# Eleven distances in the order in which two graphs' pieces are given out, and layer 3's projections as one block

## The chip, the cores and the metric

The kernel runs on one core of a Trainium2 chip. The metric is the time of one execution on the device, in microseconds (us); the median of several runs is given. A core has five engines that run side by side, each through its own queue of instructions: TensorE (PE, matrix products), VectorE (DVE), ScalarE (ACT), GpSimd (POOL) and SyncE (SP, which here issues transfers). Transfers are also issued by POOL.

## The reference

Sixteen graphs, each with 1024 nodes of 256 numbers (x) and a 1024 by 1024 adjacency, go through four graph layers. Every layer takes a normalized copy of x, cut at zero, and adds its result to x:

```python
h = jnp.maximum(_layernorm(x, axis=-1), 0.0)
x = x + layer(h, adj, ...)
```

- Layers 0 and 1 are attention with one head. h is multiplied by a weight matrix W; a logit for each edge is leaky_relu(f1[i] + f2[j]) with f1 and f2 linear in h; a softmax runs over the edges (along the first axis in layer 0, along the second in layer 1); the result is elu(attention @ (h W)).
- Layer 2 is a mean over the neighbours of h W_msg, plus h W_upd and a bias, cut at zero.
- Layer 3 is attention with four heads of 64 columns, with a bias, a cut at zero, the head's own projection added, and a normalization over each head's 64 columns.

## The kernel before, in words

**One graph.** Its nodes lie in eight tiles of 128 (NT = 8). `graph(b)` runs through the graph's stages. First come the statistics and the normalized rows of x (`Norm.pair`, four pairs of tiles): ACT writes `hn` (L667), PE transposes it (`pt_h`, L680), ACT copies it into `ht` (L681). Along with these go the mask steps: `Mask.step` turns a piece of the transposed adjacency (`raw`, loaded by SP in 256 KB pieces, L566) into bytes on ACT (L575); three pieces are loaded ahead, and each step loads another. Then, for each of the layers:

- *Layer 0* (`layer0`): eight projections (PE L686, ACT L746), each with a mask step; then a row of exponentials is spread over all partitions: a transpose `ps_col` (L699), `e_row` on ACT (L703), a transfer to DRAM (`d_row`, L705) and one back to all partitions (`row`, L711), both issued by SP. Eight tiles of attention weights `p` follow (DVE L769 and L771), and eight outputs (PE L759), each of which ACT reads twice (exponential L791, copy L793) and DVE adds to x (L736, L737, in `residual`). `residual` also gathers the sums for the next layer's norm: after every second output DVE makes `shift` (L635), ACT the squares `unread` (L640), and after every fourth POOL the inverse deviations `rs` (L592, L593).
- *Layer 1* (`layer1`): the same with projections read by ACT L802, a scaling of `hs` by ACT (L820), one DVE operation for each `p` (L822) and outputs L815, read by ACT L838 and L840.
- *Layer 2* (`layer2`): its norm needs a scale for each row; so `Norm.settle` makes `scales` on DVE (L657, L658) once `rs` is there, and only then ACT makes `hn`. This is done once before the seventh output of layer 1 (in `residual`) and once before layer 2. Eight projections are split into `hi` and `lo` (L869 to L872), and eight outputs multiply them by the adjacency (L877, L883), whose pieces POOL loads (L585).
- *Layer 3* (`layer3`): eight projections (ACT L906, and for each pair DVE L913 and L914), a wait, then four heads. A head takes one row (`row3`, of which two are held) and eight `p` (DVE L929); of each pair of `p` PE makes 32 products of 64 columns (L942). ACT reads the result (L950).
- *The tail* (`tail`): eighteen pieces, mostly DVE operations on half of the graph, two squares on ACT (L976), `rs` on POOL, and the stores.

**Two or three graphs at a time.** Every stage is a Python generator. Each `yield` gives a distance in planned units, that is, how much later the generator's next piece is given out. A queue merges the generators by these times; graph b starts at b * 120, so the heads and the tail of one graph lie among layers 0 and 1 of the next:

```python
APART = 120.0
...
while queue:
    queue.sort(key=lambda g: g[:2])
    at, b, g = queue.pop(0)
    try:
        queue.append((at + next(g), b, g))
```

`loads(b)` is a generator of its own: it issues the loads of x on POOL (`load_x`, L545, 512 KB each), and 30 units later the first three mask loads on SP. `more()` loads the weights of layers 1, 2 and 3 in the same way; those transfers are held back by `behind` (L484), a small DVE copy out of the newest layer-0 `p` of the first graph.

The order in which pieces are given out is the program's order. The framework that builds the kernel sorts the instructions of each engine's queue, with program order as the priority. Instructions marked `later` keep the program's order among themselves: all of SP's transfers, the first matmuls of layer 0's first two outputs, and some of the tail.

Of the kernel before, what the change touches and what calls it, by code (L numbers as in the profile page):

```python
# [421 lines left out]
def tile_simple_stack(  # L422
# [12 lines left out]
    B, N, D = x.shape  # L435
# [9 lines left out]
    S, S3 = 0.2, 0.01  # L445
    W3 = D + 2 * H
    HW = HO + 1
    STEP = 1.54
    EARLY = 2

    const = ctx.enter_context(tc.tile_pool(name="const", bufs=1))
# [290 lines left out]
    def layer0(b, xs, m, norm, after):  # L742
        hs = new_hs()
        for n in range(NT):
            ps = project(norm, wx[0], n, D + 2)
            nc.scalar.activation(hs[:, n, : D + 2], ps[:, : D + 2], AF.Copy, scale=norm.rs[n])  # L746
            m.step()
            yield 0.9
        mask = m.bytes
        row_a, row_b = [everywhere(d, "row") for d in spread(column(hs[:, :, D : D + 1], 1), 1, (1.0, S), "l0")]  # L750
        q = small.tile([P, NT], F32, tag="q", name="q")
        nc.scalar.activation(q, hs[:, :, D + 1], AF.Exp, scale=1.0 - S)
        watch(b, 0, hs[:, :, D : D + 2])
        yield 6.38
        ps_ = []
        early = [at_ps.tile([P, HALF], F32, tag="at", name="ps_o0") for _ in range(EARLY)]

        def product(ps, i, j):
            m = nc.tensor.matmul(  # L759
                ps[:, :D], ps_[j][:, i * P : (i + 1) * P], hs[:, j, :D], start=(j == 0), stop=(j == NT - 1)  # L760
            )
            if i < EARLY and j < 7:
                later(m)

        for j in range(NT):
            if m.raws:
                m.step(2)
            p = weights("p0")
            nc.vector.scalar_tensor_tensor(p, row_a, q[:, j : j + 1], row_b, op0=OP.mult, op1=OP.max)  # L769
            z = small.tile([P, 2], F32, tag="z", name="z", bufs=8)  # L770
            nc.vector.scalar_tensor_tensor(p, p, 1.0, mask[:, j, :], op0=OP.mult, op1=OP.mult, accum_out=z[:, 0:1])  # L771
            nc.vector.reciprocal(z[:, 1:2], z[:, 0:1])
            nc.scalar.activation(hs[:, j, :D], hs[:, j, :D], AF.Copy, scale=z[:, 1:2])  # L773
            ps_.append(p)
            if b == 0:
                gates.append(p)
            for i, ps in enumerate(early):
                if j:
                    product(ps, i, j - 1)
            yield 2.6  # L780
        for i, ps in enumerate(early):
            product(ps, i, NT - 1)
        for i in range(NT):
            if i < EARLY:
                ps = early[i]
            else:
                ps = at_ps.tile([P, HALF], F32, tag="at", name="ps_o0")
                for j in range(NT):
                    product(ps, i, j)
            e = work.tile([P, D], F32, tag="e", name="e")  # L790
            nc.scalar.activation(e, ps[:, :D], AF.Exp)  # L791
            v = work.tile([P, D], F32, tag="v", name="v")
            nc.scalar.copy(v, ps[:, :D])  # L793
            residual(xs, i, v, after, e)
            yield 3.9


    def layer1(b, xs, mask, norm, after):
        hs = new_hs()
        for n in range(NT):  # L800
            ps = project(norm, wx[1], n, D + 2)
            nc.scalar.activation(hs[:, n, : D + 2], ps[:, : D + 2], AF.Copy, scale=norm.rs[n])  # L802
            yield 1.05
        (d_row,) = spread(column(hs[:, :, D + 1 : D + 2], 1), 1, (S - 1.0,), "l1")
        row = everywhere(d_row, "row")
        watch(b, 1, hs[:, :, D : D + 2])
        q = small.tile([P, NT], F32, tag="q", name="q")
        nc.scalar.activation(q, hs[:, :, D], AF.Exp, scale=1.0 - S)
        nc.scalar.activation(hs[:, :, D], hs[:, :, D], AF.Exp, scale=S)
        yield 5.0  # L810
        ps_ = []
        early = [at_ps.tile([P, HALF], F32, tag="at", name="ps_o1") for _ in range(EARLY)]

        def product(ps, i, j):
            nc.tensor.matmul(  # L815
                ps[:, : D + 1], ps_[j][:, i * P : (i + 1) * P], hs[:, j, : D + 1], start=(j == 0), stop=(j == NT - 1)
            )

        for j in range(NT):
            nc.scalar.activation(hs[:, j, :D], hs[:, j, :D], AF.Copy, scale=hs[:, j, D : D + 1])  # L820
            p = weights("p1")
            nc.vector.scalar_tensor_tensor(p, row, q[:, j : j + 1], mask[:, j, :], op0=OP.max, op1=OP.mult)  # L822
            ps_.append(p)
            for i, ps in enumerate(early):
                product(ps, i, j)
            yield 1.3
        for i in range(NT):
            if i < EARLY:
                ps = early[i]
            else:  # L830
                ps = at_ps.tile([P, HALF], F32, tag="at", name="ps_o1")
                for j in range(NT):
                    product(ps, i, j)
            k = b * NT + i
            z = shares[:, k : k + 1]
            nc.vector.reciprocal(z, ps[:, D : D + 1])
            e = work.tile([P, D], F32, tag="e", name="e")
            nc.scalar.activation(e, ps[:, :D], AF.Exp, scale=z)  # L838
            v = work.tile([P, D], F32, tag="v", name="v")
            nc.scalar.activation(v, ps[:, :D], AF.Copy, scale=z)  # L840
            residual(xs, i, v, after, e)
            yield 3.74
# [55 lines left out]
    def layer3(b, xs, mask, norm, res):  # L898
# [5 lines left out]
        for n in range(NT):  # L904
            ps = project(norm, wx[3], n, W3)
            nc.scalar.activation(hs[:, n, :], ps[:, :W3], AF.Copy, scale=norm.rs[n])  # L906
            if n % 2:
                pair = slice(n - 1, n + 1)
                nc.scalar.activation(hbv[:, pair, :, HO], terms[:, pair, H:], AF.Exp, scale=S3)
                t = hbv[:, pair, :, :HO]  # L910
                hv = hs[:, pair, :D].rearrange("p t (h e) -> p t h e", e=HO)
                bias = rows["bias3"].rearrange("p (h e) -> p h e", e=HO).unsqueeze(1).to_broadcast([P, 2, H, HO])
                nc.vector.tensor_tensor(t, hv, bias, op=OP.add)  # L913
                nc.vector.tensor_tensor(t, t, hbv[:, pair, :, HO:].to_broadcast([P, 2, H, HO]), op=OP.mult)  # L914
            yield 1.15
        d_row = spread(column(terms[:, :, :H], H), H, (S3 - 1.0,), "l3")
        row = everywhere(d_row[0], "row3")
        watch(b, 2, terms)
# [35 lines left out]
    def tail(b, xs, hs, res):  # L954
# [4 lines left out]
        for g in range(NHALF):  # L959
# [6 lines left out]
            nc.vector.tensor_tensor(o, o, rz.unsqueeze(2).to_broadcast([P, PER * H, HO]), op=OP.mult)  # L966
            yield STEP
            nc.vector.tensor_tensor(of, of, hs[:, t, :D].rearrange("p t (h e) -> p t h e", e=HO), op=OP.add)
            yield STEP
            nc.vector.tensor_reduce(m[:, 0, :], o, axis=AX.X, op=OP.add)  # L970
            yield STEP
            total = m[:, 0, :].unsqueeze(2).to_broadcast([P, PER * H, HO])
# [10 lines left out]
        for t, o, of, m, sq in halves:  # L983
            nc.vector.tensor_reduce(m[:, 1, :], sq, axis=AX.X, op=OP.add)
            rs.append(inv_std(m[:, 1, :], PER * H, 1.0 / HO, 1e-6))
            yield STEP
        for g, (t, o, of, m, sq) in enumerate(halves):
# [18 lines left out]
    def graph(b):  # L1006
        xs = loaded.pop(b)
        m = masks.pop(b)
        norm = Norm()
        for g in range(NT // 2):  # L1010
            norm.pair(xs, g)
            m.step()
            yield 2.66
        for layer, inputs in ((layer0, (m,)), (layer1, (m.bytes,)), (layer2, ())):
            yield 2.36
            norm.settle()
            norm.flip()
            after = Norm(degrees(b) if layer is layer1 else None)
            yield from layer(b, xs, *inputs, norm, after)
            norm = after  # L1020
        yield 1.44
        norm.flip()
        res = state.tile([P, NT, H, HW], F32, tag="res", name="res", bufs=1)
        hs = yield from layer3(b, xs, m.bytes, norm, res)
        return tail(b, xs, hs, res)
# [3 lines left out]
    def loads(b):  # L1029
        loaded[b] = load_x(b)  # L1030
        yield 30.0
        masks[b] = Mask(b)
        yield 0


    APART = 120.0
    def more():

        weights01(1, w1, w1_t, a1, (1, 0))
        yield 21.6  # L1040
        weights2()
        yield 10.0
        weights3()
        yield 0

# [1 line left out]
    next(loads_0)  # L1047
    weights01(0, w0, w0_t, a0, (0, 1), wait=False)
    next(loads_0)
    queue = [(32, 0, more())] + [(b * APART, b, graph(b)) for b in range(B)] + [(b * APART - 80, b, loads(b)) for b in range(1, B)]  # L1050
    while queue:
        queue.sort(key=lambda g: g[:2])
        at, b, g = queue.pop(0)
# [86 lines left out]
```

## Time and profile before

| what | value |
|---|---|
| median of 3 runs | 2629.38 us (2628.99 to 2631.85) |
| the profiled execution | 2620.4 us, its span 2618.6 us |
| PE busy | 2473.6 us, 94% |
| DVE busy | 1965.5 us, 75% |
| ACT busy | 1448.0 us, 55% |
| POOL busy | 438.4 us, 17% |
| layer 3's `p` (L929, DVE) | 512 instructions, 1278 ns each |
| the tail's squares (L976, ACT) | 32 instructions, 1053 ns each (median) |

The profile is of one execution. Its durations add up to its own 2620.4 us, which is 9.0 us below the median of the runs. "L929" is line 929 of the kernel. "PE" is the matrix product and "PEld" the loading of its weights, which runs beside it. A wait is told as "who <- whom", with the time in total, how often, and the longest.

### The profile page before, as it was taken

The numbers are of one execution on the slowest core, as the hardware profiler recorded it, in microseconds if no ns is written. First come the engines' busy times: TensorE is split into PE (matmuls) and PEld (weight loads), VectorE is DVE, ScalarE is ACT, GpSimd is POOL, SyncE is SP. The second block draws the span as 40 slices with busy tenths as digits, with TensorE's granted clock in tenths as the row PEclk, the third lists the DMA queues.
The fourth block names the chain that finished last, engine by engine and source line by source line (L and its number), as shares of the span: only waits on it lengthen the run. The fifth ranks groups of instructions, "written<-read, shape, count | busy, mean of one in ns | idle before, by whom it ended". The sixth has DMA issues, their size and how long they took to land.

```text
span 2618.6 us, 62976 instructions
## 1 busy us (share of the span) xinstructions
PE 2473.6 (94%) x26194; PEld 2100.8 (80%) x26194; DVE 1965.5 (75%) x3815; ACT 1448.0 (55%) x4065; POOL 438.4 (17%) x454
## 2 busy tenths in 40 slices
PE   5899999999999999999999999999999999999985
PEld 4688788888878888788888878888888888878864
DVE  4357778787777877778787777977778787777858
ACT  4564755637565474755637565473755637555350
POOL 1020211203112030211202112030211203111021
PEclk7899999999999999999999999999999999999997
DMA  4531351616217161251616217161351616216021
GB/s 153 117 85 55 93 110 58 125 59 142 66 51 152 65 127 55 91 113 58 125 55 141 70 54 149 66 125 54 99 105 58 125 57 140 70 49 126 26 65 36
DMA packets 212633, 233.76 MB, mean 89 GB/s; under 512 B 10416, under 2 KB 161072, under 8 KB 212336
## 3 DMA queue, kind: packets, MB, share of 16 engines
q0 software_dynamic: 137728, 83.90, 19.4%
q1 hardware_dynamic: 74608, 145.73, 17.1%
q8 instruction: 208, 3.41, 0.5%
q14 instruction: 89, 0.73, 0.1%
HBM read 212.35 MB, written 17.24 MB: 88 GB/s over the span
## 4 chain that ended last, share of the span: by engine, by line
PE 51%; DVE 16%; ACT 15%; DMA 9%; issue 7%; POOL 2%; SPq 0%; DVEq 0%; POOLq 0%; ACTq 0%
PE ps_o L759 16%; PE ps_proj L686 11%; PE ps_o L942 11%; PE ps_o L883 6%; DVE p L929 5%; DVE p L822 4%; ACT hn L667 4%; DMA row<-d_row 3%; DMA raw<-in_adj_t 3%; ACT mask L575 2%; PE pt_h L680 2%; ACT unread L640 2%; PE ps_o L877 2%; PE ps_o L815 2%; POOL rs L593 2%
## 5 line engine op out<-in xcount | busy, mean ns | idle before, releaser
L929 DVE SCALAR_TENSOR_TENSOR p<-row,q,mask 128x1024 f32<-128x1024 f32 x512 | 632.9, 1278 | 60.8 <-PE ps_o L942 51.0
L942 PEld LDWEIGHTS ps_o<-hb,p 128*64 128x64 f32 x16384 | 506.9, 139 | 96.0 <-issue 44.7
L942 PE MATMUL ps_o<-hb,p 128*64 128x65 f32 x16384 | 544.7, 224 | 19.2 <-DVE p L929 6.1
L686 PE MATMUL ps_proj<-wx,ht 128*128 128x258 f32 (+2 forms) x2048 | 517.3, 392 | 6.5 <-ACT hs L746 5.0
L759 PE MATMUL ps_o<-hs,p 128*128 128x256 f32 x2048 | 495.6, 387 | 16.5 <-ACT hs L773 15.9
L815 PE MATMUL ps_o<-hs,p 128*128 128x257 f32 x2048 | 498.1, 390 | 13.0 <-ACT mask L575 7.4
L759 PEld LDWEIGHTS ps_o<-hs,p 128*128 128x128 f32 x2048 | 381.1, 193 | 70.2 <-ACT hs L773 21.5
L815 PEld LDWEIGHTS ps_o<-hs,p 128*128 128x128 f32 x2048 | 374.0, 191 | 69.3 <-ACT mask L575 7.6
L686 PEld LDWEIGHTS ps_proj<-wx,ht 128*128 128x128 f32 x2048 | 360.0, 190 | 85.7 <-ACT hs L746 16.0
L592 POOL TENSOR_SCALAR rs<-mv 128x4 f32<-128x4 f32 (+1 forms) x112 | 33.7, 301 | 1561.4 <-ACT unread L640 1546.8
L736 DVE SCALAR_TENSOR_TENSOR xs<-e,xs 128x256 f32<-128x256 f32 x256 | 108.0, 422 | 237.3 <-ACT e L791 164.0
L593 POOL TENSOR_TENSOR rs<-rs,neg_half 128x4 f32<-128x4 f32 (+2 forms) x144 | 257.3, 1790 | 10.7
L667 ACT ACTIVATE hn<-xs,shift 128x256 f32<-128x256 f32 x384 | 176.8, 500 | 128.3 <-DVE shift L635 126.7
L680 PE MATMUL pt_h<-ident,hn 128*128 128x128 f32 x1024 | 183.6, 285 | 37.9 <-ACT hn L667 36.5
L950 ACT ACTIVATE res<-ps_o 128x260 f32<-128x260 f32 x128 | 48.7, 381 | 298.6 <-PE ps_o L942 298.2
L883 PE MATMUL ps_o<-hi,adj 128*128 128x258 f32 x1024 | 201.2, 320 | 2.4 <-DMA adj<-in_adj 2.3
L680 PEld LDWEIGHTS pt_h<-ident,hn 128*128 128x128 f32 x1024 | 118.3, 141 | 105.6 <-ACT hn L667 85.8
L575 ACT ACTIVATE mask<-raw 128x512 uint8<-128x512 int32 x256 | 160.5, 627 | 71.8 <-DMA raw<-in_adj_t 70.6
L585 POOL DMA_DIRECT2D adj<-in_adj x128 | 114.5, 895 | 486.2 <-PE ps_o L883 452.8
L737 DVE SCALAR_TENSOR_TENSOR xs<-v,xs 128x256 f32<-128x256 f32 x384 | 160.5, 421 | 19.6 <-DVE xs L736 0.5
L769 DVE SCALAR_TENSOR_TENSOR p<-row,q 128x1024 f32<-128x1024 f32 x128 | 159.8, 1269 | 19.7 <-DMA row<-d_row 19.7
L883 PEld LDWEIGHTS ps_o<-hi,adj 128*128 128x128 f32 x1024 | 150.8, 190 | 18.3 <-DMA adj<-in_adj 4.8
(108 smaller groups left out, 3005.4 us busy)
## 6 DMA issues: line engine op xcount, KB each, us to landing
raw<-in_adj_t SPq DMA_DIRECT2D x256, 256.0 KB
adj<-in_adj POOLq DMA_DIRECT2D x128, 512.0 KB, 5.6
row<-d_row SPq DMA_DIRECT2D x112, 512.0 KB
xs<-in_x POOLq DMA_DIRECT2D x32, 512.0 KB, 7.8
out<-xs SPq DMA_DIRECT2D x32, 512.0 KB
wx<-in_w SPq DMA_DIRECT2D x3, 256.0 KB
d_row<-e_row SPq DMA_DIRECT2D x48, 4.0 KB
wts<-in_w_t SPq DMA_DIRECT2D x2, 256.0 KB
```

Source lines behind the costliest of these rows:

```text
L575: nc.scalar.activation(self.bytes[:, n, g * HALF : (g + 1) * HALF], raw, AF.Square, accum_out=squares[:, k : k + 1])
L593: nc.gpsimd.tensor_tensor(rs[:, :n], rs[:, :n], neg_half[:, :n], op=OP.pow)
L667: nc.scalar.activation(hn, xs[:, 2 * g + k, :], AF.Relu, scale=scale, bias=bias)
L680: nc.tensor.transpose(pt[:, c, k * P : (k + 1) * P], hn[:, c * P : (c + 1) * P], ident)
L686: nc.tensor.matmul(ps[:, :width], norm.ht[:, c, n * P : (n + 1) * P], w[:, c, :width], start=(c == 0), stop=(c == DC - 1))
L737: nc.vector.scalar_tensor_tensor(x, v, 0.0, x, op0=OP.max, op1=OP.add, accum_out=after.sums[:, i % 2 : i % 2 + 1])
L759: m = nc.tensor.matmul(ps[:, :D], ps_[j][:, i * P : (i + 1) * P], hs[:, j, :D], start=(j == 0), stop=(j == NT - 1))
L769: nc.vector.scalar_tensor_tensor(p, row_a, q[:, j : j + 1], row_b, op0=OP.mult, op1=OP.max)
L815: nc.tensor.matmul(ps[:, : D + 1], ps_[j][:, i * P : (i + 1) * P], hs[:, j, : D + 1], start=(j == 0), stop=(j == NT - 1))
L883: nc.tensor.matmul(ps[:, : D + 2], adj_n[j][:, i, :], h[:, i, : D + 2], start=False, stop=(h is lo and i == NT - 1), skip_group_check=True,)
L929: nc.vector.scalar_tensor_tensor(p, row, q[:, jj, h : h + 1], mask[:, jj, :], op0=OP.max, op1=OP.mult)
L942: nc.tensor.matmul(pss[g][part, k * HW : (k + 1) * HW], ps_[t][:, i * P : (i + 1) * P][:, part], hbv[:, j + t, h, :], start=(j == 0 and t ...
```

## The change

Twelve numbers are changed, eleven distances between pieces and one lead (of the loads before their graph); no operation is added or taken away. The eight projections of layer 3 are given out 0.69 apart instead of 1.15. Layer 1 waits 8.0 instead of 5.0 between its projections and its first `p`, layer 0 5.42 instead of 6.38. The other distances within the layers move by 4 to 9%. The loads of a graph are given out 60 units ahead of it instead of 80, so its first mask loads come 30 units ahead instead of 50. The weights of layers 1 to 3 start at 36 instead of 32.

```diff
@@
-    STEP = 1.54
+    STEP = 1.48
@@
-            yield 0.9
+            yield 0.98
-        yield 6.38
+        yield 5.42
@@
-            yield 2.6
+            yield 2.7
@@
-            yield 3.9
+            yield 3.74
@@
-        yield 5.0
+        yield 8.0
@@
-            yield 1.3
+            yield 1.35
@@
-            yield 1.15
+            yield 0.69
@@
-            yield 2.66
+            yield 2.55
@@
-        yield 10.0
+        yield 9.2
@@
-    queue = [(32, 0, more())] + [(b * APART, b, graph(b)) for b in range(B)] + [(b * APART - 80, b, loads(b)) for b in range(1, B)]
+    queue = [(36, 0, more())] + [(b * APART, b, graph(b)) for b in range(B)] + [(b * APART - 60, b, loads(b)) for b in range(1, B)]
```

Ahead of each pair of lines in this order: STEP (the tail), layer 0's projections, layer 0's wait for its row, layer 0's `p`, layer 0's outputs, layer 1's wait for its row, layer 1's `p`, layer 3's projections, the statistics of the first norm, the distance from layer 2's weights to layer 3's, and the queue's start (`more` and `loads`).

## The prediction

> **What bounds the kernel now.** The page comes first. TensorE (PE) is busy in 94% of the span, no other engine above 75%.
> ```profile
> PE 2473.6 (94%) x26194; PEld 2100.8 (80%) x26194; DVE 1965.5 (75%) x3815; ACT 1448.0 (55%) x4065; POOL 438.4 (17%) x454
> PE   5899999999999999999999999999999999999985
> ```
> The slices say where the rest is: two thin ones at each end, nines between. Between 130 and 2400 us the work repeats. The same matmul group starts at 1016.82 us and one graph later at 1173.8, so a graph takes 157.0 us where the queue plans 120: one planned unit is 1.31 us. The table by stages prices one such graph and its worst part.
> ```profile
> 1000.00:1157.00 157.00, 153.02 (x1638) 130.38 (x1637) 122.31 (x235) 90.23 (x254) 27.41 (x28) 1.00 0.38 92
> 1071.00:1097.00 26.00, 23.29 (x115) 17.94 (x114) 14.27 (x37) 23.32 (x59) 11.82 (x10) 1.00 0.08 24
> ```
> The first number after the span is PE's busy time, the fourth ACT's. PE is idle for 4.0 us of 157, and 2.7 of these lie in 26 us in which ACT is busy for 23.3. The list of PE's waits in this graph names the cause.
> ```profile
> PE pt_h L680 <- ACT hn L667: 2.4, 3, 1.1
> PE ps_o L759 <- ACT hs L773: 0.4, 1, 0.4
> PE ps_o L942 <- DVE shares L836: 0.3, 1, 0.3
> ```
> So 2.4 us per graph are waits of the transposes (L680) for ACT's `hn`; over 200 to 2400 us they sum to 29.9 us. The timelines of PE and of ACT show two of the three.
> ```profile
> 1078.51 0.44 PE L680 MATMUL pt_h<-ident,hn 128*128 128x128 f32 x2 [0.85 <-ACT hn L667]
> 1082.26 0.44 PE L680 MATMUL pt_h<-ident,hn 128*128 128x128 f32 x2 [1.15 <-ACT hn L667]
> ```
> ```profile
> 1077.85 0.60 ACT L667 ACTIVATE hn<-xs,scales 128x256 f32<-128x256 f32 x1
> 1078.36 1.04 ACT L976 ACTIVATE sq<-res 128x1024 f32<-128x1024 f32 x1
> ...
> 1081.61 0.59 ACT L667 ACTIVATE hn<-xs,scales 128x256 f32<-128x256 f32 x1
> ```
> These are `settle` before the seventh layer-1 output. Between two `hn` that PE waits for, ACT does a square of the other graph's tail (L976, 0.95 us to the next start), a mask step, two squares of the norm, and the exponential and copy of an output.
> A second loss is hidden in PE's busy time: changing over between layer 3's 64-column matmuls and others.
> ```profile
> 1053.60 2.09 PE L942 MATMUL ps_o<-hb,p 128*64 128x65 f32 x64
> 1055.61 1.14 PE L815 MATMUL ps_o<-hs,p 128*128 128x257 f32 x4
> 1062.64 7.20 PE L815 MATMUL ps_o<-hs,p 128*128 128x257 f32 x32
> ```
> Correcting the eye: a block of 32 takes 7.04 us up to the next start, 0.22 each; four alone take 1.07 instead of 0.88. A visit costs 0.2 to 0.3 us. Some ten such pairs lie in a graph, over 2 us.
>
> **What the Trainium skill says.** "TensorEngine Tiling (Array Packing)", Key Properties, says that changing the tiling mode drains TensorE. The 0.19 us above agrees, and gives the price. "Perfetto Trace Analysis", Identifying the Most-Contended Engine, warns that matmul busy time does not show the distance to the limit; PE's 94% beside weight loads of 80% agrees. Its Optimization Strategy says to interleave regimes with different bounds: here layer 3's heads (1030 to 1062 us: DVE busy 31.3 of 32 us) and the ACT-bound part above. "DMA: Bandwidth & Descriptors", Issuing engines are not separate DMA queues, says that transfers issued by different engines share 16 engines; below, moved loads can slow a row.
>
> **The change part by part.** No instruction is added or removed. The distances set the order in which pieces are given out, and the trace shows that this is a priority and not the order run: the next graph's statistics, given out over 8 planned units, run together at 1059 to 1061 us. Only what `later` marks, all of SP's transfers among it, keeps its order. So each edit is priced by which pieces change places. Positions are planned units after a graph's start.
>
> *Tail and layer-1 outputs (STEP, layer-0 and layer-1 distances, layer 3's block).* A graph's layer 3 now ends at 235.26 instead of 236.78, the tail's two squares come at 121.18 and 127.10 of the next graph (before 122.94 and 129.10), and layer 1's seventh output, with its `settle`, at 129.34 (before 127.18). The second square was 1.92 units behind `settle` and is now 2.24 ahead. That takes its 0.95 us out from between the two `hn`, where PE waits 1.15 us. I take 0.9 us per graph saved; at most both waits (2.0) go; if mask steps take the place it is 0.
>
> *Changes of tile.* In the queue's order, after layer 1's row, layer 3's heads give way to layer 1 seven times instead of eight: one visit, 0.3 us saved (0 to 0.6).
>
> *Layer 1's row, 5.0 to 8.0.* Three more units of layer 3 alone, about one step of 64 matmuls. DVE makes its two p at 1.2 us each, 2.4, and PE uses them in 2.02: 0.4 us lost per graph (0 to 0.8). The wait was tight: row issued at 1032.64, first p of L822 at 1037.1 with DVE never idle.
>
> *Loads, 80 to 60.* Mask loads go on SP from behind head 0's row (three issues of 0.4 us and 768 KB, ahead of head 1's row) to behind layer 1's row, ahead of head 3's. Nothing of SP waits for them: their buffers have been free since the fourteenth to sixteenth mask step, and the first use is some 20 us later. Layer 1's row then lands beside them. In graph 0, where its issue at 103.3 is followed by three mask loads, p begins 4.7 us later; the longer wait (3.9 us more) covers that. Head 3's row is used some 12 us after its issue. Price 0 on both sides; if the row is late by 1 us, DVE has the heads' p to do. The x loads on POOL ran as soon as a buffer was free (graph 2's, given out at 160, is issued at 62 us), so their place among the adjacency loads and the rs operations (two issues of 0.8 us) should hardly move. If they did, waits for the adjacency, 2.3 us of PE in 200 to 2400, bound the gain at 0.15 per graph; as 1 MB in front of head 0's row it would be hidden by 7 us of layer-0 outputs.
>
> *Layer 3's projections as a block; layer 0's 0.98, 5.42, 2.7 and 3.74; the norm's 2.55.* From 1132 to 1157 us PE is busy for 25.00 of 25 us: no wait to remove. Layer-0 and layer-3 projections and outputs have the same tile, so regrouping costs no change. Row 3 starts 1.5 units earlier behind the same outputs. Layer 0's shorter wait lets DVE stand before L769 for its row (1.2 us per graph now) with layer 2's additions behind it; PSUM is emptied by ACT there, so PE does not see it. 0, with 0.4 either way.
>
> *The start.* `more` at 36 gates layer 1's weights on the fourth p instead of the third. In the trace the gate's copies (45.6 us) already stand behind both, so 0; a pair later would be up to 5 us once, PE's wait for `avs` (4.4 us) the other way. Layer 2's and 3's weights wait on the eighth p either way. The last graph runs alone and in the same order: 0.
>
> *Sum.* -0.9 - 0.3 + 0.4 = -0.8 us per graph; with up to 0.1 for the freer head-0 row -0.9, on 15 graphs that meet a neighbour: -13.5 us. The profiled execution took 2620.4 us (span 2618.6 and 1.8 around it), 9.0 below the median of 2629.38. 2620.4 - 13.5 = 2606.9, and 9.0 more for the median: 2616.
>
> **The rivals.** *Slower: the late last output.* Layer 1's last output moves from 10.92 to 13.08 in the next graph's time, while the layer-0 projections that cover what follows it start at 12.56 instead of 13.0. From the last output's matmuls (end 1083.9) to the transposes of layer 2's second half (1094.7) runs a chain DVE, ACT, POOL (rs, 1.9 us), DVE, ACT; PE fills it with eight projections of 0.88 us, four of layer 2, and loses 1.3 us. The change moves the projections 2.6 units, 3.4 us, ahead against that output. Half of this lost is some 2.0 us: -0.9 + 2.0 = +1.1 per graph, 15 times: 2629.4 + 16.5 = 2646. It decides from about one projection (0.9 us) run too early. For it: ACT is full there. Against: layer 2's start moves 2.16 units with the output.
> *No difference.* As only priorities move, the scheduler may place ready work as before, or gain and loss cancel: 2629. The batch of statistics speaks for it; against it, SP's order must change.
> *More than forecast.* Both `settle` waits go (2.0) and half of the 1.3 us: -2.5 per graph with the rest, -37: 2592. ACT is idle for 45% of the span, so there is room elsewhere.
>
> **How the numbers follow.** A measurement of this kernel tells about 0.2% (5 us) from no change. The forecast gets 0.42, more than forecast 0.16, no difference 0.15, slower 0.27. Faster 0.58, same 0.15, slower 0.27. The range goes from 2592 to 2645, nearly to the slower rival's value. The likeliest side alone spans 2592 to 2624.
>
> **What would show it.** Right: the waits of L680 for `hn` fall from 2.4 to about 1.5 us per graph, with L976 no longer between the two scaled `hn`; the period falls from 157.0 to about 156.1; the three mask loads stand behind layer 1's row; ten or fewer changes between L942 and L815. Wrong: the period is longer, with PE waiting for `hn` or `hs` between 1084 and 1098 us of such a graph (the slower rival); DVE waits for the row before L822; or the ends, not the period, carry the difference.

## The result, and the profile after

The change makes no difference that the runs can tell: 2628.57 us (median of four, 2621.43 to 2632.52) against 2629.32 (median of four). The ratio of the runs, which here and below is worked out from all of them and not from the two medians, is 0.9992, with a 95% interval from 0.9968 to 1.0016. The forecast was 2616. The profiled execution took 2621.43 us (span 2619.6), 1.0 more than that of before.

The busy times on the page of the changed kernel:

```profile
PE 2456.4 (94%) x26194; PEld 2094.9 (80%) x26194; DVE 1965.3 (75%) x3815; ACT 1439.9 (55%) x4065; POOL 449.5 (17%) x454
```

PE is busy for 17.2 us less than before in a span that is no shorter. Its work became denser, and the time came back as idle time. The table by stages, in the two windows of before (columns: span, then PE, PEld, DVE, ACT, POOL busy, clock, DMA share, GB/s), shows it in one graph: PE 1.1 us less busy in 157.

```profile
1000.00:1157.00 157.00, 151.89 (x1635) 129.65 (x1634) 121.85 (x234) 89.61 (x254) 28.20 (x28) 1.00 0.36 91
1071.00:1097.00 26.00, 23.26 (x116) 18.16 (x115) 17.42 (x43) 23.00 (x58) 12.02 (x10) 1.00 0.19 62
```

The list of PE's waits in this graph (in total, times, longest):

```profile
PE pt_h L680 <- ACT hn L667: 2.6, 2, 2.1
PE ps_o L942 <- DVE p L929: 1.0, 2, 0.7
PE ps_o L759 <- ACT hs L773: 0.6, 1, 0.6
```

The 2.4 us that were to become 1.5 are 2.6; two waits for `p` and one for layer 0's `hs` stand beside them. PE's and ACT's timelines show what became of the place that the forecast was about.

```profile
1074.11 0.44 PE L680 MATMUL pt_h<-ident,hn 128*128 128x128 f32 x2 [2.06 <-ACT hn L667]
```
```profile
1068.59 1.06 ACT L976 ACTIVATE sq<-res 128x1024 f32<-128x1024 f32 x1
...
1073.55 1.31 ACT L667 ACTIVATE hn<-xs,shift 128x256 f32<-128x256 f32 x3
...
1075.22 1.06 ACT L976 ACTIVATE sq<-res 128x1024 f32<-128x1024 f32 x1
...
1078.16 0.61 ACT L667 ACTIVATE hn<-xs,scales 128x256 f32<-128x256 f32 x1
...
1080.97 0.61 ACT L667 ACTIVATE hn<-xs,scales 128x256 f32<-128x256 f32 x1
```

Both squares now stand ahead of both `hn` with `scales`, as foretold, and the waits of 0.85 and 1.15 us for those are gone. One wait of 2.06 us has come instead: for an `hn` of the *next graph's* first norm (input `shift`), which stands on ACT behind the first square, three mask steps, a copy of `ht`, two squares of a norm and the exponential and copy of an output.

The other graphs show the same. PE's timelines, sorted by the input of the `hn` that ended each wait, give for 200 to 2400 us: before the seventh output PE waited 20.7 us for an `hn` with `scales` in the kernel before (22 times) and not once in the changed one, and in the changed one it waits 17.6 us a few us ahead of there for an `hn` with `shift` (once in each of 14 graphs), which it did not before.

To see a whole run and not one graph I averaged over 13 graphs of each trace: the period, PE's idle times over 0.15 us by the kind of matmul that follows, and the rest, which is PE's time above a fixed pace of each kind (for example 0.216 us for an output of layer 0, 0.0315 for a product of layer 3). In us per graph (of one execution of each kernel; the runs of the kernel before differ among themselves by up to 15 us, about 1 us per graph):

```
                     before   after   change
period               157.07  156.99   -0.08
waits before:
  transposes (hn)      2.15    2.07   -0.08
  layer 3              0.84    1.46   +0.62
  layer 0              0.22    0.90   +0.68
  projections          0.28    0.00   -0.28
  layers 1 and 2       0.51    0.33   -0.18
rest                   7.90    7.08   -0.82
  of which changes between layer 3 and others: 3.31 (30) -> 3.18 (28)
```

So gain and loss of about 1.3 us each meet: layer 3's and layer 0's waits grow by 1.30, all else falls by 1.36. One of the waits for layer 3 in PE's timeline:

```profile
1050.86 2.09 PE L942 MATMUL ps_o<-hb,p 128*64 128x65 f32 x64 [0.68 <-DVE p L929]
```

### The profile page after: what moved, and what is told of

Same layout as the page of the kernel before. It is cut to its first block, busy times and chain, and to the rows that moved or that the text cites. A ratio compares the mean times of both kernels' runs of the same rounds, so it can differ in the third digit from the quotient of the medians.

```text
span 2619.6 us, 63024 instructions
## 1 busy us (share of the span) xinstructions
PE 2456.4 (94%) x26194; PEld 2094.9 (80%) x26194; DVE 1965.3 (75%) x3815; ACT 1439.9 (55%) x4065; POOL 449.5 (17%) x454
## 4 chain that ended last, share of the span: by engine, by line
PE 56%; DVE 16%; DMA 12%; ACT 11%; issue 3%; POOL 2%; SPq 0%; DVEq 0%; POOLq 0%; ACTq 0%
PE ps_o L759 15%; PE ps_proj L686 12%; PE ps_o L942 9%; DVE p L929 6%; PE ps_o L883 6%; PE ps_o L815 6%; DMA row<-d_row 5%; PE pt_h L680 5%; DMA raw<-in_adj_t 4%; DVE p L822 4%; ACT mask L575 3%; PE ps_o L877 3%; ACT hn L667 2%; DMA d_row<-e_row 2%; ACT unread L640 2%
## 5 line engine op out<-in xcount | busy, mean ns | idle before, releaser
L929 DVE SCALAR_TENSOR_TENSOR p<-row,q,mask 128x1024 f32<-128x1024 f32 x512 | 631.9, 1278 | 65.4 <-PE ps_o L942 55.7
L942 PEld LDWEIGHTS ps_o<-hb,p 128*64 128x64 f32 x16384 | 505.5, 138 | 102.0 <-DVE p L929 41.2
L942 PE MATMUL ps_o<-hb,p 128*64 128x65 f32 x16384 | 541.6, 224 | 28.9 <-DVE p L929 20.8
L759 PE MATMUL ps_o<-hs,p 128*128 128x256 f32 x2048 | 494.0, 386 | 26.4 <-ACT hs L773 26.0
L686 PE MATMUL ps_proj<-wx,ht 128*128 128x258 f32 (+2 forms) x2048 | 507.8, 388 | 4.0 <-ACT hs L746 2.3
L759 PEld LDWEIGHTS ps_o<-hs,p 128*128 128x128 f32 x2048 | 379.7, 191 | 82.8 <-ACT hs L773 30.3
L686 PEld LDWEIGHTS ps_proj<-wx,ht 128*128 128x128 f32 x2048 | 365.8, 190 | 79.6 <-ACT hs L746 10.4
L592 POOL TENSOR_SCALAR rs<-mv 128x4 f32<-128x4 f32 (+1 forms) x112 | 40.6, 362 | 1555.3 <-ACT unread L640 1542.1
L769 DVE SCALAR_TENSOR_TENSOR p<-row,q 128x1024 f32<-128x1024 f32 x128 | 161.4, 1270 | 25.1 <-DMA row<-d_row 25.1
L822 DVE SCALAR_TENSOR_TENSOR p<-row,q,mask 128x1024 f32<-128x1024 f32 x128 | 156.9, 1279 | 10.3 <-DMA row<-d_row 10.1
```

The lines of the kernel that those rows point to most:

```text
L686: nc.tensor.matmul(ps[:, :width], norm.ht[:, c, n * P : (n + 1) * P], w[:, c, :width], start=(c == 0), stop=(c == DC - 1))
L759: m = nc.tensor.matmul(ps[:, :D], ps_[j][:, i * P : (i + 1) * P], hs[:, j, :D], start=(j == 0), stop=(j == NT - 1))
L929: nc.vector.scalar_tensor_tensor(p, row, q[:, jj, h : h + 1], mask[:, jj, :], op0=OP.max, op1=OP.mult)
L942: nc.tensor.matmul(pss[g][part, k * HW : (k + 1) * HW], ps_[t][:, i * P : (i + 1) * P][:, part], hbv[:, j + t, h, :], start=(j == 0 and t ...
```

## The experiments

All ratios are against the kernel before on the same chip, with a 95% interval. The waits given in each are of PE, summed over 200 to 2400 us of its trace unless said otherwise; in that stretch before and after compare as follows.

Of before:

```profile
PE pt_h L680 <- ACT hn L667: 29.9, 41, 1.3
PE ps_o L759 <- ACT hs L773: 2.9, 7, 0.7
```

Of after:

```profile
PE pt_h L680 <- ACT hn L667: 28.6, 32, 2.1
PE ps_o L942 <- DVE p L929: 13.5, 26, 0.7
PE ps_o L759 <- ACT hs L773: 12.0, 14, 1.8
```

### What holds hn up: square, mask steps, or ACT's load

**The tail's squares on DVE** (`b_sqdve`, kernel before).

```diff
-            nc.scalar.activation(sq, o, AF.Square)
+            nc.vector.tensor_tensor(sq, o, o, op=OP.mult)
```

> The kernel before with the tail's two squares (L976) made by DVE instead of ACT, so that none stands between the hn before settle, wherever the pieces are given out. Square theory (the forecast's step): PE's wait for hn falls from 2.15 to about 1.2 us per graph, 13 us faster, 2616 us. Load theory (ACT is simply full in the 26 us around the last layer-1 outputs, 90%, and PE waits whatever stands there): two of its 23.3 us go, the wait falls by some 0.3 to 0.5 us per graph at most, 2622 to 2629 us. Against both: DVE, with 2.4 us per graph more, delays the layer-1 outputs, 2635 us.

Measured: 2640.11 us, 1.0039 [1.0022, 1.0057]. The waits for `hn` rose from 29.9 to 48.6 us. In the graph at 1072 to 1086 us a DVE square stood between the two operations that make `scales` (L657 at 1081.33, L658 at 1082.88), so it held up the same `hn` from the other side. Moving the square to DVE therefore does not tell whether the square was the cause.

**No squares at all** (`b_nosq`, kernel before; L976 is left out, and the reduction behind it reads the values that were to be squared).

```diff
-            sq = work.tile([P, N], F32, tag="p3", name="sq", bufs=5).rearrange("p (k e) -> p k e", e=HO)
-            nc.scalar.activation(sq, o, AF.Square)
-            halves.append((t, o, of, m, sq))
+            halves.append((t, o, of, m, o))
```

> The kernel before without the tail's two squares: L976 is left out and the reduction after it (L984) reads the centred values instead, so the deviations of layer 3 are wrong. This takes the square out of ACT without putting it on DVE, where it stood between the two operations that make scales. Square theory (the forecast's): PE's wait for hn falls from 2.15 to about 1.2 us per graph, 13 us faster, 2616 us. Chain theory (the wait is set by where the scheduler puts the transposes against a chain ACT, POOL, DVE, ACT whose length it underrates, and stays near 2 us whatever single piece is moved): the wait stays between 1.7 and 2.5 us per graph, 2625 to 2632 us.

Measured: 2623.03 us, 0.9983 [0.9971, 0.9995]. Even with 32 squares gone and ACT 26 us less busy, the waits did not fall:

```profile
PE pt_h L680 <- ACT hn L667: 40.7, 51, 2.1
```

The waits in the very place, before the seventh output for an `hn` with `scales`, were 22.8 us (28 times) against 20.7. So the square was in front of `hn`, but leaving it out does not take the wait away. The kernel gained 0.17%, about 4.5 us, and not through this wait. The idea behind the forecast's first step falls here.

**Mask steps in the program's order** (`b_masklater`, kernel before). In both kernels ACT's mask steps stand ahead of `hn` while their piece is not there yet (44.9 us of ACT idle in the kernel before).

```diff
-                nc.scalar.activation(
+                later(nc.scalar.activation(
                     self.bytes[:, n, g * HALF : (g + 1) * HALF], raw, AF.Square, accum_out=squares[:, k : k + 1]
-                )
+                ))
```

> The kernel before with the mask operation pinned behind ACT's previous instruction in program order, so that mask steps no longer run ahead of the norm's hn; no other edit. Mask theory (PE's wait of the transposes for hn is made by mask steps that stand ahead of it in ACT's queue and wait for their loads): ACT's idle time before mask operations falls from 70.6 us in the whole run to under 30, PE's wait for hn from 2.15 to about 1.0 us per graph, the time by 15 us to 2614. Square theory (the forecast's: the tail's square between the hn makes it): the wait stays at 2.1 us per graph, 2629 us. Against both: the masks come late for layer 0's p and PE waits there, slower than 2635.

Measured: 2659.54 us, 1.0113 [1.0096, 1.013]. ACT's idle time for the masks' pieces fell to 0.2 us, and it helped nothing: PE waited 32.3 us for `hn` and 11.4 us for layer 0's projections to be read, which was 4.0 before.

```profile
PE ps_proj L686 <- ACT hs L746: 11.4, 14, 0.8
```

**Half of the copies of ht off ACT** (`b_htdve`, kernel before; the copies for the first norm and for layer 2, 128 of 256, go to DVE. `first` is set for the first norm alone).

```diff
-            nc.scalar.copy(self.ht[:, :, g * 2 * P : (g + 1) * 2 * P], pt)
+            part = self.ht[:, :, g * 2 * P : (g + 1) * 2 * P]
+            if self.times is not None or self.first:
+                nc.vector.tensor_copy(part, pt)
+            else:
+                nc.scalar.copy(part, pt)
```

> The kernel before with the copy of the transposes into ht made by DVE instead of ACT, for the first norm and layer 2's norm alone (eight copies of 0.57 us per graph, all of them in or near the ACT-bound part). Load theory: ACT's busy time there falls from 23.3 to about 19 of 26 us, PE's wait for hn from 2.15 to under 1.2 us per graph, 14 us faster, 2615 us. Rival (the wait is made by the chain's latency and not by ACT's load): the wait stays near 2 us, 2629 us or slower, as a DVE copy can stand behind 1.2 us operations.

Measured: 2649.02 us, 1.0063 [1.0038, 1.0088]. ACT was busy for 52 us less in the whole run (1395.8 instead of 1448.0), and the waits for `hn` were 51.9 us, the most of all. In the part that the forecast called ACT-bound ACT had become free (the fourth busy time), but PE had not gained:

```profile
1071.00:1097.00 26.00, 22.67 (x106) 18.90 (x103) 17.95 (x39) 17.83 (x49) 10.06 (x8) 0.87 0.29 91
```

So less work on ACT does not by itself shorten the waits; `b_nosq`, which gives DVE nothing in exchange, says the same. What is left, argued and not tested: each of these edits gave the scheduler another order, and in each PE's transposes came to stand in front of an `hn` that was not ready.

The line shows a second loss, which no list of waits has: a granted clock of 0.87. In this trace PE's clock was granted at one half in twelve stretches of 3.4 or 6.8 us between 200 and 2400 us, 44 us in all; in the 3.4 us ahead of each PE had been idle for 1.9 to 3.0 us. The traces of before and after have no such stretch there. PE was busy for 42 us of the 44; at full speed that work would have taken 21, so by this estimate they cost up to 21 us, which is more than the 17 us by which the kernel is slower. `b_masklater` has seven stretches (24 us) and `b_sqdve` three (10 us).

### Layer 0's and layer 1's waits, and the loads

**Layer 0's wait alone, layer 1's wait alone** (`b_l0wait`, `b_l1wait`: kernel before with 5.42 for 6.38, and with 8.0 for 5.0).

> The kernel before with only layer 0's wait for its row cut from 6.38 to 5.42. Trade theory (the change gains 0.8 us per graph in changeovers and short waits and loses it in two new waits, one of them made by this number): PE's wait of layer 0's matmuls for the scaled hs rises from 0.22 to about 0.9 us per graph, and the time by 14 x 0.7 = 10 us, to 2639 us. Rival (this wait comes from layer 2's outputs, which also moved): it stays near 0.2, and the time stays at 2629 us. Rival (something other than PE holds the 157 us period): the wait moves and the time does not.

> The kernel before with only layer 1's wait for its row widened from 5.0 to 8.0. Trade theory: PE's waits of layer 3's products for DVE's p rise from 0 to about 1 us per graph, the changeovers between layer 3 and others fall by one or two visits of 0.3 us; sum +0.4 to +0.7 us per graph, 2635 to 2639 us. Rival (the p waits come from layer 3's earlier heads or the moved mask loads): no new p wait, the time stays at 2629 us or falls to 2624.

Measured: layer 0's wait 2642.37, 1.0053 [1.0034, 1.0073]; layer 1's 2629.18, 0.9994 [0.9983, 1.0006]. With 5.42 PE's waits for layer 0's `hs` rose from 2.9 to 7.8 us, and the waits for `hn` changed place as in the changed kernel (for `scales` 26.0 to 8.9 us, for `shift` 3.9 to 23.4). With 8.0 PE's waits rose by 0.11 us per graph at layer 3, 0.53 at layer 1 and 0.49 at layer 2's updates, and 0.7 went elsewhere, 0.43 of it in the rest; the period of its profiled execution is 157.48 us (+0.41), but the runs show no loss.

**Both old waits in the changed kernel** (`a_bothwaits`: 6.38 and 5.0 back).

> The changed kernel with the two waits put back (layer 0's to 6.38, layer 1's to 5.0), the other ten numbers as changed. Trade theory: the two new waits of PE (0.7 us per graph for layer 0's hs, up to 1.0 for layer 3's p) go and the gains stay: 14 x 1.2 = 17 us faster than the changed kernel, about 2612 us. Rival (the period is held by another engine or by the loads): 2629 us again. Rival (the gains need the wide layer-1 wait): waits and changeovers both return to those of before, 2627 us.

Measured: 2682.38, 1.0194 [1.0177, 1.0211]. DVE waits for the row before layer 1's `p` (12.5 us, 13 times; 0.9 in the kernel before). That is the row that now has the mask loads behind it on SP. PE's waits for layer 0's `hs` were 18.2 us though layer 0's wait was 6.38 again.

**The loads and layer 1's wait together** (`b_loads_l1wait`: kernel before with 60 and 8.0).

```diff
-        yield 5.0
+        yield 8.0
...
-... [(b * APART - 80, b, loads(b)) for b in range(1, B)]
+... [(b * APART - 60, b, loads(b)) for b in range(1, B)]
```

> The kernel before with two of the twelve numbers changed: the loads' lead 60 instead of 80, and layer 1's wait 8.0 instead of 5.0. Pair theory (the wide wait is there to cover the mask loads that now stand behind layer 1's row, and neither gives anything without the other numbers): within 0.2% of before, 2625 to 2634 us, no wait of layer 1's products for p above 0.4 us per graph. Rival (the mask loads behind layer 1's row cost even with the wide wait): DVE waits for the row before L822, slower by 0.5% or more, 2643 us.

Measured: 2630.37, 1.0003 [0.9992, 1.0015]. Together the two cost nothing. That is the price of 0 that the prediction gave the loads behind a longer wait.

**Layer 0's four numbers: alone, and taken back** (`b_layer0`: 0.98, 5.42, 2.7, 3.74 in the kernel before; `a_layer0`: the old ones in the changed kernel).

> The kernel before with layer 0's four distances as changed (0.98, 5.42, 2.7, 3.74) and nothing else. Sum theory (layer 0's four numbers cost what putting them back won on the changed kernel): 0.25 to 0.5% slower, 2636 to 2642 us, PE's wait of layer 0's matmuls for hs up from 0.22 to about 0.9 us per graph. Joint theory (a number's worth depends on the others): within 0.1% of before or faster.

> The changed kernel with layer 0's four distances put back (0.9, 6.38, 2.6, 3.9), the other eight as changed. Sum theory (parts add up: layer 0's shorter wait alone cost 0.5%, so without it the rest must gain as much): about 2615 us, PE's wait of layer 0's matmuls for hs back at 0.2 us per graph. Joint theory (the numbers fit each other only as a set): slower than the changed kernel by 0.5% or more, 2642 us, with layer 0's wait above 0.9 us per graph.

Measured: alone 2637.58, 1.003 [1.0019, 1.0041]; taken back 2622.06, 0.9968 [0.9957, 0.9979]. They cost 0.3% in one setting; in the other the difference is 0.24% (0.9968 to 0.9992), but the two intervals overlap. The wait that was expected to show the cost does not show it: in the kernel before with these four numbers PE waits 0.7 us for layer 0's `hs`, less than the 2.9 without them, and the waits on its list sum to no more than before (54 us against 55). PE's busy time is 16.5 us longer (2490.1). Where the 0.3% comes from stays open.

In the changed kernel without them PE's waits are:

```profile
PE pt_h L680 <- ACT hn L667: 16.1, 29, 1.5
PE ps_col L699 <- DVE scales L658: 16.1, 14, 1.1
```

Layer 0's 12.0 us have left the list. Of the 12.5 us that `hn` lost, more than all came back at the transpose of the column (L699), a wait that the profile puts down to `scales` on DVE.

### Layer 3's projections as a block

**Alone, and taken back as well** (`b_l3block`: 0.69 in the kernel before; `a_layer0_l3`: 1.15 in the changed kernel that has layer 0's old numbers).

```diff
-            yield 1.15
+            yield 0.69
```

> The kernel before with layer 3's projections given out 0.69 apart instead of 1.15 and nothing else. The forecast's step (no cost and no gain, 0.4 us per graph either way): 2629 us, between 2623 and 2635. Block theory (this is what makes the eight numbers other than layer 0's gain 0.3%): 2621 us, with fewer changeovers or shorter waits. Rival (heads that start 1.5 units earlier meet layer 0's outputs): slower, 2638 us.

> The changed kernel with layer 0's four distances and layer 3's projections put back; what is left changed is the tail's, layer 1's and the first norm's distances, the loads and the weights. Block theory (layer 3's block makes the 0.3% that remained without layer 0's numbers): back to 2629 us. Rival (the tail's and layer 1's numbers make it): 2622 us, with PE's wait for hn near 1.2 us per graph as without layer 0's numbers alone. Joint theory: neither, slower than 2634.

Measured: alone 2729.5, 1.0376 [1.0355, 1.0397]; taken back 2633.98, 1.0017 [1.0007, 1.0028], so that with the rest of the change but layer 0's numbers the block *gains* 0.5% (1.0017 to 0.9968). The block alone fills the lists with waits (DVE's and PE's lines):

```profile
DVE st L631 <- DMA xs<-in_x: 47.7, 13, 5.4
PE ps_o L759 <- ACT hs L773: 29.8, 12, 3.9
DVE p L822 <- DMA row<-d_row: 27.3, 13, 3.4
PE ps_o L942 <- DVE p L929: 25.5, 30, 1.3
```

The first one is a surprise: the statistics of the next graph wait for its x. Timelines of POOL, DVE and PE:

```profile
1147.06 1.59 POOL L545 DMA_DIRECT2D xs<-in_x  x2 [13.44 <-DMA d_row<-e_row]
```
```profile
1155.23 1.08 DVE L631 BATCH_NORM_STATS2 st<-xs 128x6 f32<-128x256 f32 x3 [4.83 <-DMA xs<-in_x]
...
1157.56 2.47 DVE L769 SCALAR_TENSOR_TENSOR p<-row,q 128x1024 f32<-128x1024 f32 x2
```
```profile
1162.99 3.32 PE L759 MATMUL ps_o<-hs,p 128*128 128x256 f32 x8 [2.90 <-ACT hs L773]
```

The x load is issued 4.4 us after the tail's last store (SP, 1142.63), and only 8 us before the statistics begin; which transfer POOL waited for is not certain, as the profile names the one that came last. Behind them on DVE stand layer 0's eight `p`, whose row was issued at 1147.2; PE then waits 2.90 us for what follows from the first. The eight products behind that wait take 3.32 us, where the pace of 0.216 makes 1.7; the clock (the column after POOL's busy time) was granted at one half meanwhile:

```profile
1163.50:1166.90 3.40, 3.40 (x12) 2.69 (x10) 3.40 (x9) 2.66 (x9) 0.00 (x0) 0.50 0.05 6
```

There are fourteen such stretches in 200 to 2400 us, 65 us long, and PE had been idle for 1.9 to 3.4 of the 3.4 us ahead of each. By the same estimate as above they are up to 29 of the 100 us that the block costs. The waits on PE's list grew from 55 to 139 us.

The built program has this order in it. On DVE, from one graph's tail on, with X for its two last additions (L1002), l for L872, S for the first four of the next graph's eight statistics (L631), a for layer 0's `p` (L769):

```
before                    X llll X ll aaaaaaaa SSSS
block alone               X ll X llllll SSSS aaaaaaaa
block, wait of 8.0        X ll X llllll aaaaaaaa SSSS
block, loads at 60        X ll X llllll SSSS aaaaaaaa
changed                   X l X lllllll aaaaaaaa SSSS
changed, both old waits   X ll X llllll SSSS aaaaaaaa
```

Four runs take this apart; all are the kernel before with the block and more.

**Loads at 60 and layer 1's wait of 8.0** (`b_l3_pair`).

> Kernel before with three numbers of the change: layer 3's projections 0.69 apart, loads 60 units ahead, layer 1's wait 8.0. Statistics theory: layer 3's block alone cost 3.8% because the first four statistics of the next graph (L631) stood in DVE's queue ahead of this graph's eight layer-0 p, where they wait for an x load that is issued only after the tail's stores (DVE waited 4.8 us for xs in the graph at 1000 to 1165 us). In the program's order of this kernel they stand behind the eight p again, so the cost is gone: 2616 to 2632 us. Rival, heads theory: the block is dear by itself, because layer 3's heads are given out 3.7 units earlier against layer 1's p and outputs; then at least 1.5% remains, over 2670 us.

Measured: 2625.63, 0.9984 [0.9975, 0.9992]. DVE no longer waits for x at all. The heads theory falls.

**The tail's step of 1.48** (`b_l3_step`).

> Kernel before with layer 3's projections 0.69 apart and the tail's step 1.48. Statistics theory: a faster tail stores its x about one unit earlier, but in the program's order the four statistics still stand ahead of layer 0's p, so DVE still waits for the x load: 2690 us or more. Rival, store theory: the x load is only late because it waits for the tail's last store, and an earlier tail repairs that: under 2650 us. Heads theory: as alone, about 2725.

Measured: 2719.45, 1.0342 [1.0324, 1.036]. Here x comes nearly in time: 8.6 us of waits for it instead of 47.7. The cost stays, in other places (PE's line; the waits for layer 1's row are 24.4 us):

```profile
PE ps_o L942 <- DVE p L929: 34.4, 37, 2.5
```

So the store theory falls, and with it the part of the statistics theory that put the cost on the waiting for x. What stays is that kernels with this order are slow.

**The wait of 8.0 without the loads, the loads without the wait** (`b_l3_l1wait`, `b_l3_loads`).

> Kernel before with layer 3's block and layer 1's wait of 8.0, loads at 80. In the program's order on DVE the four statistics stand behind layer 0's p, as in the kernel before. Order theory: the wait alone repairs the block, 2617 to 2635 us. Rival, loads theory: the loads at 60 repaired it in the run with both; then 2680 us or more remains.

> Kernel before with layer 3's block and loads at 60, layer 1's wait 5.0. In the program's order on DVE the four statistics stand ahead of layer 0's p, as with the block alone. Order theory: 2670 us or more, as the block alone (2729) or the changed kernel with both old waits (2682), which has the same order. Rival, loads theory: the loads at 60 alone repair the block, 2617 to 2635 us.

Measured: with the wait 2628.4, 0.9994 [0.9986, 1.0003]; with the loads 2729.42, 1.0385 [1.0366, 1.0404]. Layer 1's wait alone repairs the block. With it the same part of DVE's timeline reads:

```profile
1129.34 1.27 DVE L769 SCALAR_TENSOR_TENSOR p<-row,q 128x1024 f32<-128x1024 f32 x1
1132.63 1.39 DVE L631 BATCH_NORM_STATS2 st<-xs 128x6 f32<-128x256 f32 x4
```

The four statistics come last, without a wait, 20.7 us after the x load's issue (1111.92). The waits of L759 for `hs` are 2.0 us and those of L942 for `p` 6.2, against 29.8 and 25.5.

All four kernels seen with the statistics in front of layer 0's `p` cost 1.9 to 3.9%, and none with them behind costs over 1.2%. As the edits change nothing but the order, the order as a whole is the cause, and the last two runs show that layer 1's wait decides it. That it is the place of these four instructions and not another difference between the two orders was not tried. One such rival stands open: in the four slow kernels DVE also waits 12.5 to 27.3 us for layer 1's row, in all others at most 5.8, and a longer wait gives that row more time.

### The tail's step, and the fastest set

**Block, loads, layer 1's wait and the tail's step** (`b_l3_pair_step`), and **the changed kernel with the old step** (`a_step`, 1.54).

> Kernel before with the block, the loads at 60, layer 1's wait 8.0 and the tail's step 1.48; four of the seven distances by which the fastest kernel so far (changed, with layer 0's four numbers back, 2622.1) differs from before. Statistics theory: these four carry all of its gain: 2617 to 2626 us. Rival: the three others (layer 1's p 1.35, the norm's 2.55, the weights at the start) are needed, 2628 or more.

> Changed kernel with the tail's step 1.54 back. The prediction's working put the square's move ahead of settle down to STEP and layer 1's distances together. In this program's order on ACT both squares still stand where they stand in the changed kernel, ahead of the scaled hn, so the order theory expects no difference: 2624 to 2633 us, PE's wait for hn again about 2.1 us per graph. Rival: the tail's step is what holds the changed kernel together, 2640 or more, or what costs it its gain, 2618 or less.

Measured: the four together 2623.33, 0.9968 [0.9959, 0.9977]; the changed kernel with the old step 2625.68, 0.9986 [0.9978, 0.9995]. The four carry all the gain of `a_layer0`; the numbers that these two differ in (layer 1's `p`, the first norm, the weights at the start) bring nothing that the runs can tell. The step brings 0.16% in one setting (0.9984 to 0.9968) and nothing to be told in the other. `a_step` had more waits for `hn` than expected (43.8 us, 3.15 a graph) and was no slower for it.

Put in a row, the ratios to before are:

```
layer 1's wait                       0.9994   0.9983 to 1.0006
  + block                            0.9994   0.9986 to 1.0003
    + loads                          0.9984   0.9975 to 0.9992
      + tail's step                  0.9968   0.9959 to 0.9977
        + layer 1's p, norm, start   0.9968   0.9957 to 0.9979
          + layer 0's four numbers   0.9992   0.9968 to 1.0016   (the change)
```

`b_l3_pair_step` and `a_layer0` beat the kernel before by 0.3%. Their medians lie 5 to 6.5 us under that of the changed kernel, but the three were not measured in one series, and its own interval reaches down to theirs.

## Why the prediction was wrong, point by point

- **The tail's square (-0.9 per graph): the step that failed.** The move happened as foretold, and the waits beside it went in every graph: 20.7 us in all, 1.5 per graph, more than was forecast. But 17.6 us, 1.25 per graph, came back a few us ahead of that place, for an `hn` of the next graph's first norm, and the waits for `hn` as a whole fell by 0.08 us. The step priced the wait that goes and put nothing for one that comes. It also took the operation between two `hn` for the cause of the wait, and `b_nosq` speaks against that: no square, and 22.8 us of waits in that place instead of 20.7. The order of ACT and that of PE both changed, so a wait can go without the time going with it; what set the new wait was not tested. The step named its own lower bound ("if mask steps take the place it is 0"), and that is nearly what came: three mask steps and the first square stand before the `hn` of the 2.06 us.
- **Changes of tile (-0.3): right in kind, half in size.** PE goes from layer 3 to layer 1 eight instead of ten times per graph. The time lost between layer 3 and others fell by 0.13 us.
- **Layer 1's row wait (+0.4): the size of the waits was right, their place only in part, the time not.** Layer 3's waits grew by 0.62 us per graph in the changed kernel. With the wait alone those of layers 1 and 3 together grew by 0.64, but 0.53 of it are layer 1's. The bound was 0.8. Alone, though, the runs show no loss (0.9994).
- **Loads (0): right, with the wait.** The mask loads went behind layer 1's row, as the timeline of SP's queue (SPq) shows, and the pair costs nothing (1.0003). One reading was off: in graph 0 the row is issued at 103.29 and the first `p` starts at 107.72, 4.4 us later and not 4.7.

```profile
1030.70 0.32 SPq L711 DMA_DIRECT2D row<-d_row  x1
1031.07 1.37 SPq L566 DMA_DIRECT2D raw<-in_adj_t  x3
1032.55 0.38 SPq L711 DMA_DIRECT2D row<-d_row  x1
```

- **Layer 0's numbers (in the term "0, with 0.4 either way"): the second term mis-sized.** They cost 0.30% alone, 7.9 us, 0.5 per graph over 15; within the change the medians differ by 6.5 us (2628.57 less 2622.06), which the runs do not tell from nothing. The working said that PSUM (where PE puts its results) is emptied by ACT and PE does not see DVE standing before L769. In the changed kernel PE waits more behind it: DVE's waits for layer 0's row rose from 11.8 to 17.1 us, and PE's for `hs` from 2.9 to 12.0; without the four numbers the latter are 0.2. But with the four alone DVE waits 15.4 us for that row and PE 0.7 for `hs`, and in `a_step`, which has them too, PE waits 0.3. So this is not shown to be how they cost time.
- **Layer 3's block (in the same term): a price that holds only in company.** With layer 1's wait it is 0 (0.9994 and 0.9994), with the loads as well -0.19% (1.0003 to 0.9984, -0.3 us per graph). Alone it is +3.8%, nearly 7 us per graph. The prediction priced it by asking whether PE waits where it is done. What it can do to the order of another graph's statistics is seen in no view of the kernel before.
- **What the sum left out.** The rest fell by 0.82 us per graph, of which 0.13 are layer 3's changes. No term stood for the other 0.7.
- **The rivals.** "Gain and loss cancel", given 0.15, is what the waits show. Four distances bring 0.3% in a set of their own; that layer 0's four take it back fits the medians, but the interval of the change is too wide to show it. The slower rival did not come: between 1084 and 1098 us PE waits 0.6 us, not 2. Its starting loss of 1.3 us is not in the profile of before, which has PE busy for 10.43 of the 10.80 us from 1083.9 to 1094.7. "More than forecast" had both `settle` waits going; they went, and another came.

## What to carry to other kernels

Where a scheduler turns a given order into the one that runs, an operation seen in front of a late one is not yet its cause: leave it out in a run, and see whether the wait goes, before a gain is put on it. Distances between pieces have no price of their own: one of them was worth +3.8%, 0 and -0.5% in three settings, so they are tried in the sets in which they belong together, and a part that costs when tried alone (here layer 0's) is left out. The place of far-off instructions in each engine's queue is compared first; a change of order there told the slow kernels from the others, though it was not shown which instruction made them slow. And a slow kernel's granted clock is read stage by stage: in these traces every stretch at half the clock in the middle of a run came behind waits of PE.

## What was not expected

- PE's waits for `hn` and the time of the kernel hardly go together: 40.7 us of waits at 0.9983, 43.8 at 0.9986, 16.1 at 0.9968, 6.8 at 1.0017, and 29.9 in the kernel before.
- Taking work from ACT, the engine that PE waits for most, and giving it to DVE made the kernel slower twice (52 us less: +0.63%; 26 us less, with the squares on DVE: +0.39%). DVE was busy for 72.8 and 30.9 us more in these two.
- PE's granted clock fell to one half in the middle of runs in which PE is busy for over 90% of the time. In the kernel before it did not, though single waits there last up to 2.0 us; the stretches of `b_masklater` follow 1.2 to 2.0 us of idle time in 3.4. How much idle time it takes was not tried.
